# A two-layer graph kernel on one core: layer 0 of the first eight batches with plain weight blocks, factor sums of the q, k, v weights in other tiles, first loads from two queues

## The chip, the cores and the metric

The kernel runs on one core of a Trainium2 chip. The metric is the device time of one execution in microseconds (us); lower is better. A core has a matrix engine (TensorE, in the profile PE, with its weight loads shown as PEld), VectorE (DVE), ScalarE (ACT), GpSimd (POOL) and SyncE (SP). Each has its own queue of instructions and works through it strictly in order. SP does no arithmetic here: it issues transfers (DMAs), which 16 DMA engines carry out. An instruction that waits holds up everything behind it in its queue.

## The reference

128 batches of a 128x512 matrix go through two layers. `adj` is a 128x128 matrix shared by all batches.

```python
# layer 0
h = relu(layernorm(x))                                # x: (128, 128, 512) f32
x = x + (einsum('nm,bmd->bnd', adj, h) @ weight + bias)
# layer 1: masked attention with 8 heads of 64, projection, norm, two residuals
h = relu(layernorm(x))
q, k, v = split(h @ w_qkv)
p = softmax(where(adj == 0, -inf, q @ k.T / 8))
o = (p @ v) @ w_proj + b_proj
x = x + o + layernorm(o) * ln_gamma + ln_beta
```

All of it is float32.

## The kernel before

**Tiling.** A batch is one 128x512 tile. Layer 0 and the projection work on pairs of batches, the q, k, v products on groups of four, attention on single batches. The big products (`x @ weight`, `x @ w_qkv`, `x @ w_proj`) are done by a Strassen-Winograd scheme: the two-by-two block product takes seven block products instead of eight, and in return needs four sums of blocks on the left ("left factors", `left_factors`, on POOL: `ysum` for layer 0, `hsum` for q, k, v, `osum` for the projection) and four on the right ("factor sums" of the weights). `seven` runs the seven products as a generator, one per step of the plan. In layer 0 a block product is two matmuls of 128x128 by 128x256 for a pair of batches; in q, k, v it is four.

**The weights.** `w0_sb` and `wp_sb` hold seven blocks each, four loaded and three more, with one of the loaded ones overwritten, made by `combine_square` (four subtractions). The twelve factor sums of `w_qkv` do not stay in SBUF: `combine_qkv` loads the four blocks of one kind (q, k or v), forms four sums and writes them to DRAM (`SUMS`). `fetch` later brings the weight block of each product (a plain block from `w_qkv` or a sum from `SUMS`) into one of five `wq` buffers.

**The stages of a pair.** `load` (x into one of six buffers); `norm0` (statistics on DVE, a power on POOL, `relu` on ACT, and POOL adds the bias `b0` into x); `mix` (four small matmuls with the transposed `adj`, copied to `yT` by ACT); `pair_left`; `layer0` (seven products, results added to x by DVE straight from PSUM, giving x1); `norm1` (statistics, relu on ACT, then `exchange`: the tile goes to DRAM as `d` and comes back as `h1x` in four strips per batch, so that `flip`, a DVE transpose in 32x32 blocks, gives the full transpose `h1T`); `keep_x1` (POOL adds `beta`, SP stores x1 to DRAM); `group_left` and `qkv` for four batches; `scores`, softmax, a second exchange, `attend`, `project`, `finish`.

**What sets the order.** The order is written out by hand: `put(t, f, ...)` pushes every step with a key t on one heap, and the loop at the end pops the steps in order of t and emits their instructions. t is a planned time, but only the order matters: each engine gets its instructions in the order in which they are emitted. In the steady part a batch has a slot of 17.8 (`SLOT`, `when`). Slots below -3 (`BEGIN`) are squeezed to 7.0 each (`FILL`), which places the first layer 0 pairs, the sums of the weights and the loads ahead of slot 0. All transfers are issued by SP.

**The lines around the change.** Loads and weight blocks: L74, L81, L95, L98. `combine_square`: L102 to L105 (DVE for `w0_sb`, POOL for `wp_sb`). `combine_qkv`: loads L131, stores L136. `fetch`: L144. Power: L182. Exchange: out L195, back L200. Left factors: L209. Adding products from PSUM: L238 and L281. `relu` L249, bias L252, `mix` L261, layer 0 products L275, norm1's relu L300, `keep_x1` L307 and L309, `flip` L316, q, k, v products L344 with the copies L348, scores L364. The results of `combine_qkv` lie in tiles that attention uses later (`sx`, `pT`, `s`, `e`), the same ones for each of the three kinds.

Of the kernel before, what the change touches and what calls it, by code (L numbers as in the profile page):

```python
# [9 lines left out]
F32 = mybir.dt.float32  # L10
AF = mybir.ActivationFunctionType
ALU = mybir.AluOpType
AX = mybir.AxisListType

P = 128
# [5 lines left out]
def kernel(  # L21
# [71 lines left out]
    def load_square(w_sb, w):  # L93
        for k, row, col in ((0, 0, 0), (4, 0, F), (5, 1, 0), (3, 1, F)):
            nc.sync.dma_start(out=w_sb[:, k], in_=block(w, row, col))  # L95

    def broadcast(t, src):
        nc.sync.dma_start(out=t, in_=src.partition_broadcast(P))  # L98

    def combine(eng, b11, b12, b21, b22, t1, t2, t3, t4):  # L100

        eng.tensor_tensor(t1, b12, b11, op=ALU.subtract)  # L102
        eng.tensor_tensor(t2, b22, t1, op=ALU.subtract)
        eng.tensor_tensor(t3, b22, b12, op=ALU.subtract)
        eng.tensor_tensor(t4, b21, t2, op=ALU.subtract)  # L105
# [19 lines left out]
    def combine_qkv(t, kind):  # L125

        bs, ts = ([work.tile([P, 2, 2, F], F32, name=n, bufs=bufs) for n, bufs in names]
                  for names in ((("sx", 1), ("pT", 2)), (("s", 2), ("e", 1))))
        bs, ts = ([t_[:, n] for t_ in ts_ for n in range(2)] for ts_ in (bs, ts))
        for n, b in enumerate(bs):  # L130
            nc.sync.dma_start(out=b, in_=qkv_block(kind, n // 2, n % 2))  # L131

        def sums():
            combine(nc.vector, *bs, *ts)
            for k, t_ in zip((1, 2, 4, 6), ts):
                nc.sync.dma_start(out=SUMS[kind, k], in_=t_)  # L136

        put(t, sums)

    def fetch(g, kind, k):  # L140

# [129 lines left out]
    def pair_chain(left, w_sb, tiles, addend, x, y):  # L271

        def product(k, p, first, last):
            for c in range(2):
                nc.tensor.matmul(p[:, 0, :], lhsT=left[k][:, c, :], rhs=w_sb[:, k, c, :], start=first and c == 0,  # L275
                                 stop=last and c == 1, skip_group_check=True)

        results = [t[:, n * F:(n + 1) * F] for t in tiles for n in range(2)]

        def start(n, p):  # L280
            nc.vector.tensor_tensor(results[n], p[:, 0, :], addend[n // 2][:, n % 2 * F:(n % 2 + 1) * F], op=ALU.add)  # L281

        return seven({"x": x, "y": y, "z": "at"}, product, start, results, [1.0] * 7)

    def layer0(j):
        for b in (2 * j, 2 * j + 1):
# [29 lines left out]
        nc.vector.transpose(H1T[g][:, :, j, :].rearrange("p c (q r) -> p q c r", q=Q),  # L316
                            H1.pop(i).rearrange("p q (c r) -> p q c r", c=C))

    def group_left(g, t):

        h = H1T.pop(g)
        LEFT1[g] = left_factors(t, 4, h[:, 0:2, 0:2, :], h[:, 2:4, 0:2, :], h[:, 0:2, 2:4, :], h[:, 2:4, 2:4, :], "hsum")

    def qkv(g, kind):

# [121 lines left out]

    SLOT, FILL = 17.8, 7.0  # L450
    BEGIN, LAST = -3, B - G
    later, count = [], [0]

    def put(t, f, *a):
# [1 line left out]
        heapq.heappush(later, (t, count[0], f, a))  # L456

    def when(i, us):
        if i < BEGIN:
            return BEGIN * SLOT + (i - BEGIN + us / SLOT) * FILL  # L460
        return i * SLOT + us

    def run(make, times):

# [23 lines left out]
            return when(i, 0.5)  # L488
        return scores_at(i) + 3

    def h0_at(i):
        return when(i - 11 - i % 2, 13.2 if i % 2 else 12)

    def read_at(i):
        return when(i + 1, 9) if i < LAST and i % 2 else 0

# [16 lines left out]
    for i in range(-11, B):  # L513
        stage(when(i, 0), load, i + 13)
        t = when(i, (11.6, 9.2)[i % 2])
        stage(t, mix, i + 10, t)
        if i % 2:
            stage(t - 4, norm0, (i + 11) // 2, t - 4, bound=B // 2)
        if i >= 0:
            put(scores_at(i), scores, i, scores_at(i))  # L520
            put(flip_at(i), flip_probs, i)
            put(attend_at(i), attend, i, attend_at(i))

    idle = when(LAST, 13)
    for j in range(B // 2):
        a, b = 2 * j, 2 * j + 1
        i = a - 8
        t = when(i - 1, 12)
        put(t, pair_left, j, t, 2.5, YT, LEFT0, "ysum")
        run(lambda j=j: layer0(j), [when(i, p) for p in PAIR[0]])  # L530
        t = when(i, PAIR[0][6]) + 1.5
        put(t, norm1, j, t)
        put(when(i + 2, 7.5), flip, a)
        put(when(i + 2, 9), flip, b)
# [12 lines left out]
        put(end - 7, reload, a)  # L547
        put(end - 4, reload, b)
        put(end, finish, j, end)

    steps = []
    for g in range(B // G):
        i = g * G - 3
        put(when(i - 1, 13), group_left, g, when(i - 1, 13))
# [49 lines left out]
```

## Time and profile before

| what | value |
|---|---|
| time, median of 3 runs | 2447.01 us (2442.28 to 2448.1) |
| the profiled execution's own time | 2436.75 us |
| its span | 2435.0 us |
| busy: PE, PEld, DVE, ACT, POOL (us of the span) | 2338.9, 2051.1, 1617.8, 1043.9, 1681.7 |
| transfers on SP's queue | 521.89 MB, 66.9% of the 16 DMA engines' time |

All numbers but the first row come from one profiled execution. The page cuts the span into 40 slices: PE is at 90% or more in all of them but the first two and the last two. Idle time of another engine costs nothing by itself; idle time of PE does. The instructions in the rows are counted as the hardware runs them: a float32 matmul appears twice, so that one block product of layer 0 (two matmuls) is "x4" in a row and one of q, k, v (four matmuls) is "x8".

### The profile page before, as it was taken

The page shows a single profiled execution, that of the slowest core. Times are in us where ns is not written, and L with a number is a line of the kernel's source. Part 1 is how long each engine was busy: PE and PEld are TensorE (multiplying, and loading weights), DVE is VectorE, ACT ScalarE, POOL GpSimd, SP SyncE. Part 2 cuts the span into 40 slices and gives each one's busy share as a digit, 9 for nine tenths or more (in the row PEclk, how much of TensorE's full clock was granted, in tenths as well). Part 3 has the DMA queues.
Part 4 walks back from the last instruction along what each step waited for, and adds up shares of the span by engine and source line. Part 5 has one row for each costly group of instructions (what it writes and reads, how often), then busy time and mean ns, then how long its engine had stood idle before and what let it go on. Part 6 is the DMA issues. An engine that isn't in the chain of part 4 may idle for free.

```text
span 2435.0 us, 42720 instructions
## 1 busy us (share of the span) xinstructions
PE 2338.9 (96%) x14081; PEld 2051.1 (84%) x14081; DVE 1617.8 (66%) x3255; ACT 1043.9 (43%) x3074; POOL 1681.7 (69%) x1610
## 2 busy tenths in 40 slices
PE   4699999999999999999999999999999999999985
PEld 3588888888888888888888888888888888888873
DVE  4466667667667667677677677666766766766554
ACT  2144444444444444445444444444444444444432
POOL 3356776777867767867767777777777676776657
PEclk8899999999999999999999999999999999999998
DMA  4666776676677676667676676677667667667653
GB/s 161 212 217 217 229 225 216 222 227 214 227 228 221 221 226 215 221 224 224 219 230 215 222 228 219 215 227 230 216 221 228 224 210 229 219 217 227 207 161 109
DMA packets 400076, 524.62 MB, mean 215 GB/s; under 512 B 40048, under 2 KB 250096, under 8 KB 399856
## 3 DMA queue, kind: packets, MB, share of 16 engines
q1 hardware_dynamic: 399856, 521.89, 66.9%
q8 instruction: 113, 1.85, 0.3%
q14 instruction: 107, 0.88, 0.1%
HBM read 350.81 MB, written 170.92 MB: 214 GB/s over the span
## 4 chain that ended last, share of the span: by engine, by line
PE 88%; DMA 3%; DVE 3%; POOL 2%; issue 2%; SPq 1%; ACT 1%; POOLq 0%; DVEq 0%; ACTq 0%
PE pc L344 38%; PE pd L275 25%; PE pz L344 6%; PE ps L364 5%; PE po L411 5%; PE pmix L261 4%; PE pz L275 4%; DMA sx<-d 2%; SPq L200 1%; DVE pT L402 1%; ACT e L387 1%; DMA wq<-in_L_gnn_w_qkv_dram 0%; DMA pT<-in_L_gnn_w_qkv_dram 0%; DVE s L372 0%; DVE st L177 0%
## 5 line engine op out<-in xcount | busy, mean ns | idle before, releaser
L182 POOL TENSOR_TENSOR rs<-ve,minus_half 128x2 f32<-128x2 f32 x192 | 133.7, 696 | 660.8 <-DVE ve L180 573.4
L344 PE MATMUL pc<-hsum,wq 128*128 128x256 f32 x2048 | 485.1, 380 | 10.5 <-POOL hsum L209 5.3
L387 ACT ACTIVATE e<-s,mx 128x128 f32<-128x128 f32 x1024 | 397.0, 389 | 189.0 <-DVE mx L378 94.3
L344 PEld LDWEIGHTS pc<-hsum,wq 128*128 128x128 f32 x2048 | 388.8, 190 | 66.5 <-POOL hsum L209 6.9
L275 PE MATMUL pd<-w_sb,ysum 128*128 128x256 f32 x1024 | 267.8, 385 | 37.1 <-DVE x L281 31.5
L275 PE MATMUL pd<-wp_sb,osum 128*128 128x256 f32 x1024 | 265.7, 383 | 8.6 <-POOL osum L209 4.2
L396 POOL TENSOR_TENSOR e<-e,sm 128x1024 f32<-128x1024 f32 x128 | 244.9, 1913 | 29.8 <-DVE sm L395 24.1
L275 PEld LDWEIGHTS pd<-w_sb,ysum 128*128 128x128 f32 x1024 | 192.2, 193 | 63.9 <-issue 27.9
L344 PE MATMUL pc<-h1T,wq 128*128 128x256 f32 x1024 | 245.1, 382 | 0.0
L344 PE MATMUL pc<-wq,hsum 128*128 128x256 f32 x1024 | 244.9, 382 | 0.0
L574 ACT COPY oT<-po 128x512 f32<-128x512 f32 x128 | 74.9, 585 | 384.0 <-PE po L411 383.9
L402 DVE STREAM_TRANSPOSE pT<-sx 128x1024 f32<-128x1024 f32 x128 | 158.4, 1238 | 106.3 <-DMA sx<-d 106.3
L275 PEld LDWEIGHTS pd<-wp_sb,osum 128*128 128x128 f32 x1024 | 190.8, 192 | 35.1 <-POOL osum L209 7.3
L344 PEld LDWEIGHTS pc<-wq,hsum 128*128 128x128 f32 x1024 | 191.7, 190 | 29.2 <-ACT v L348 0.3
L344 PEld LDWEIGHTS pc<-h1T,wq 128*128 128x128 f32 x1024 | 191.9, 190 | 28.9 <-DMA wq<-in_L_gnn_w_qkv_dram 0.4
L372 DVE TENSOR_TENSOR s<-ps,maskb 128x512 f32<-128x512 f32 x256 | 159.2, 684 | 58.7 <-PE ps L364 58.7
L348 ACT COPY qkT<-pc 128x512 f32<-128x512 f32 x256 | 144.1, 574 | 118.9 <-PE pc L344 118.6
L437 ACT ACTIVATE t<-o,shift,rs 128x512 f32<-128x512 f32 x128 | 103.1, 807 | 206.6 <-DVE shift L186 204.9
L387 ACT ACTIVATION_READ_ACCUMULATOR e<-s,mx 128x1 f32 x1024 | 191.5, 187 | 0.0
L432 POOL TENSOR_TENSOR x1b<-x1b,o 128x512 f32<-128x512 f32 x128 | 162.7, 1271 | 21.1 <-DMA x1b<-x1d 19.1
L281 DVE TENSOR_TENSOR o<-pd,bp_b 128x256 f32<-128x256 f32 x256 | 106.3, 415 | 106.6 <-PE pd L275 106.1
L438 POOL TENSOR_TENSOR t<-t,gamma_b 128x512 f32<-128x512 f32 x128 | 162.9, 1272 | 18.7 <-ACT t L437 18.7
(83 smaller groups left out, 4702.6 us busy)
## 6 DMA issues: line engine op xcount, KB each, us to landing
wq<-wt SPq DMA_DIRECT2D x384, 256.0 KB, 3.8
wq<-in_L_gnn_w_qkv_dram SPq DMA_DIRECT2D x288, 256.0 KB, 3.5
d<-e SPq DMA_DIRECT2D x128, 512.0 KB, 2.9
sx<-d SPq DMA_DIRECT2D x512, 128.0 KB, 2.9
x<-in_x_dram SPq DMA_DIRECT2D x130, 256.0 KB, 4.3
d<-h SPq DMA_DIRECT2D x128, 256.0 KB, 2.9
x1d<-x SPq DMA_DIRECT2D x128, 256.0 KB, 3.1
h1x<-d SPq DMA_DIRECT2D x512, 64.0 KB, 2.2
```

Source lines behind the costliest of these rows:

```text
L182: nc.gpsimd.tensor_tensor(rs, ve, minus_half, op=ALU.pow)
L275: nc.tensor.matmul(p[:, 0, :], lhsT=left[k][:, c, :], rhs=w_sb[:, k, c, :], start=first and c == 0, stop=last and c == 1, skip_group_check ...
L344: nc.tensor.matmul(p[:, half, :], lhsT=lhsT, rhs=rhs, start=first and half == 0 and c == 0, stop=last and c == 1, skip_group_check=True)
L348: nc.scalar.copy(results[n], p)
L364: nc.tensor.matmul(ps[e][:, c, :], lhsT=qk[r, c, j % 2, :], rhs=qk[r, C + c, j % 2, :], start=True, stop=True)
L372: nc.vector.tensor_tensor(s[:, e * C:(e + 1) * C, :], ps[e], m4, op=ALU.add)
L387: nc.scalar.activation(e[:, :, h, :], s[:, h, :].rearrange("p (q r) -> p q r", q=Q), AF.Exp, bias=shift[:, h:h + 1], scale=scale, accum_ou ...
L396: nc.gpsimd.tensor_tensor(e, e, sm.unsqueeze(1).unsqueeze(3).to_broadcast([P, Q, H, R]), op=ALU.mult)
L402: nc.vector.transpose(PT[i].rearrange("p h (q r) -> p q h r", q=Q), S.pop(i).rearrange("p q (h r) -> p q h r", h=H))
L411: nc.tensor.matmul(p[e * HD:(e + 1) * HD, c, :], lhsT=v[:, h:h + HD], rhs=PT[i][:, e * C + c, :], start=True, stop=True)
L432: put(t + 1 + 3 * n, lambda i=i: nc.gpsimd.tensor_tensor(X1B[i], X1B[i], O[i], op=ALU.add))
L438: put(t + 1.5, lambda: nc.gpsimd.tensor_tensor(n, n, gamma_b, op=ALU.mult))
```

## The change

Layer 0 of batches 0 to 7 (`AHEAD = 8`) no longer goes through the seven products of a pair. A new function `layer0_whole` takes one batch at a time: eight matmuls with the four plain blocks of `weight` into one PSUM bank (`d0` or `d1` in turn), and a single 128x512 add on DVE. These batches need no left factors and no factor sums of `weight`, so `combine_square` of `w0_sb` moves from DVE at the start to POOL ahead of pair 4.

The plan's start is laid out anew: `START` is the key of the first `mix`, the eight batches follow at a `STEP` of 4.3, and slots below 0 are 9.6 long (`SHORT`). `combine_qkv` is split: the loads are emitted 12 ahead of the sums, each sum is a step of its own followed by its store, and each of the three kinds has its own tiles (kind 0 `sx`, `pT`, `s`, `e`; kind 1 `pT`, `s`, `o`; kind 2 `oT`, `x1b`, `t`). `adj`, the four blocks of `weight` and the bias are issued from ACT's queue instead of SP's. The load and the combination of `wp_sb`, and the broadcasts of `b_proj` and `gamma`, move from before slot 0 to slots 0 to 2. From batch 8 on, the keys of the stages are those of before.

```diff
-    nc.sync.dma_start(out=adj_sb, in_=adj)
+    nc.scalar.dma_start(out=adj_sb, in_=adj)
...
+    BLOCKS = (0, 4), (5, 3)
+    def load_square(eng, w_sb, w):
+        for row, places in enumerate(BLOCKS):
+            for col, k in enumerate(places):
+                eng.dma_start(out=w_sb[:, k], in_=block(w, row, col * F))
...
-    load_square(w0_sb, w0)
+    load_square(nc.scalar, w0_sb, w0)
     for i in range(2, 4):
         load(i)
-    broadcast(b0_b, b0)
+    broadcast(nc.scalar, b0_b, b0)
...
+    def load_qkv(kind, *names):
...
+        for n in range(4):
+            nc.sync.dma_start(out=pieces[n], in_=qkv_block(kind, n // 2, n % 2))
+        return pieces
+    def combine_qkv(eng, t, kind, pieces):
+        bs, ts = pieces[:4], pieces[4:8]
+        for n, (k, first, second) in enumerate(((1, 1, 0), (2, 3, None), (4, 3, 1), (6, 2, None))):
+            second = bs[second] if second is not None else ts[n // 2]
+            put(t + 1.5 * n, combine_one, eng, SUMS[kind, k], ts[n], bs[first], second)
+    def combine_one(eng, d, t, a, b):
+        eng.tensor_tensor(t, a, b, op=ALU.subtract)
+        nc.sync.dma_start(out=d, in_=t)
...
-            put(h0_at(i) + 2, bias, X[i])
+            put(h0_at(i) + (6 if i < AHEAD else 2), bias, X[i])
...
+    def layer0_whole(i, t):
+        p = psum.tile([P, 2, F], F32, tag=f"d{i % 2}", name=f"pd{i % 2}", bufs=1)
+        y = YT[i // 2] if i % 2 == 0 else YT.pop(i // 2)
+        for c in range(C):
+            for col in range(2):
+                nc.tensor.matmul(p[:, col, :], lhsT=y[:, c, i % 2, :], rhs=w0_sb[:, BLOCKS[c // 2][col], c % 2, :],
+                                 start=c == 0 and col == 0, stop=c == C - 1, skip_group_check=True)
+        X1[i] = work.tile([P, D], F32, name="x1", bufs=3)
+        put(t + 3.6, lambda: nc.vector.tensor_tensor(X1[i], p.rearrange("p a f -> p (a f)"), X.pop(i), op=ALU.add))
...
-    SLOT, FILL = 17.8, 7.0
-    BEGIN, LAST = -3, B - G
+    SLOT, SHORT, STEP = 17.8, 9.6, 4.3
+    BEGIN, LAST, AHEAD = -3, B - G, 8
+    START = BEGIN * SHORT - 38.5
...
+        return i * SLOT + us if i >= 0 else i * SHORT + us * SHORT / SLOT
+    def mix_at(i):
+        return START + i * STEP if i < AHEAD else when(i - 10, (11.6, 9.2)[i % 2])
+    def h0_at(i):
+        return mix_at(i) - 1.2 if i < AHEAD else when(i - 11 - i % 2, 13.2 if i % 2 else 12)
...
+            put(START - 3 + i if i < 6 else mix_at(i - 6) + 10 if i < AHEAD + 6 else when(i - 13, 0), load, i)
...
+        if a < AHEAD:
+            t = mix_at(a) - 5
+            put(t, norm0, j, t)
+            for n in (a, b):
+                t = mix_at(n) + 5.2
+                put(t, layer0_whole, n, t)
+            t += 4.4
+            flips = t + 11.7, t + 12.7
+        else:
...
+            put(t, pair_left, j, t, 2.5, YT, LEFT0, "ysum")
+            run(lambda j=j: layer0(j), [when(i, p) for p in PAIR[0]])
...
-    put(when(-10, 5), combine_square, nc.vector, w0_sb)
-    put(when(-10, 4), turn_adj)
-    put(when(-8, 16), make_mask)
-    for kind, t in enumerate((when(-9, 4), when(-4, 0), when(-2, 2))):
-        put(t, combine_qkv, t + 7, kind)
-    put(when(-6, 9), load_square, wp_sb, w_proj)
-    for t, src in ((beta_b, beta), (bp_b, b_proj), (gamma_b, gamma)):
-        put(when(-8, 9), broadcast, t, src)
-    put(when(-1, 9), combine_square, nc.gpsimd, wp_sb)
+    put(START - 6, turn_adj)
+    put(when(-2, 2), make_mask)
+    for kind, (t, tiles) in enumerate((
+            (START + 25, (("sx", 1, [P, Q, H * R]), ("pT", 2, [P, 2 * C, P]), ("s", 2, [P, 2 * C, P]), ("e", 1, [P, Q, H, R]))),
+            (START + 37, (("pT", 2, [P, 2 * C, P]), ("s", 2, [P, 2 * C, P])) + (("o", 4, [P, D]),) * 4),
+            (START + 48, (("oT", 2, [P, C, 2, P]),) * 2 + (("x1b", 2, [P, D]),) * 2 + (("t", 2, [P, D]),) * 2))):
+        put(t - 12, lambda kind=kind, t=t, tiles=tiles: combine_qkv(nc.vector, t, kind, load_qkv(kind, *tiles)))
+    put(when(-2, 9), combine_square, nc.gpsimd, w0_sb)
+    put(START + 8, broadcast, nc.sync, beta_b, beta)
+    put(when(0, 12), load_square, nc.sync, wp_sb, w_proj)
+    put(when(1, 3), broadcast, nc.sync, bp_b, b_proj)
+    put(when(1, 4), broadcast, nc.sync, gamma_b, gamma)
+    put(when(2, 12), combine_square, nc.gpsimd, wp_sb)
```

More of the change, by code (lines that the diff above doesn't have):

```diff
@@ L91, in block, with broadcast @@
         return w[row * F:(row + 1) * F, col:col + F].rearrange("(c p) o -> p c o", p=P)
[L93 to L98, printed above, removed]
+    BLOCKS = (0, 4), (5, 3)
[3 more added lines that the diff above has]
+                eng.dma_start(out=w_sb[:, k], in_=block(w, row, col * F))
+    def broadcast(eng, t, src):
+        eng.dma_start(out=t, in_=src.partition_broadcast(P))
     def combine(eng, b11, b12, b21, b22, t1, t2, t3, t4):
@@ L123 @@
     SUMS = {(kind, k): dram.tile([P, 2, F], F32, name=f"wt{kind}{k}", bufs=1) for kind in KINDS for k in (1, 2, 4, 6)}
[L125 to L138, printed above, removed]
+    def load_qkv(kind, *names):
+        pieces = []
+        for name, bufs, shape in names:
+            t = work.tile(shape, F32, name=name, bufs=bufs)
+            t = t if len(shape) == 2 else t.rearrange("p a b -> p (a b)") if len(shape) == 3 else \
+                t.rearrange("p a b c -> p (a b c)")
+            pieces += [t[:, n:n + D].rearrange("p (c o) -> p c o", c=2) for n in range(0, t.shape[1], D)]
+        for n in range(4):
[9 more added lines that the diff above has]
+        nc.sync.dma_start(out=d, in_=t)
     def fetch(g, kind, k):
@@ L317, in flip, with group_left @@
                             H1.pop(i).rearrange("p q (c r) -> p q c r", c=C))
-    def group_left(g, t):
+    def group_left(g, t, gap):
         h = H1T.pop(g)
-        LEFT1[g] = left_factors(t, 4, h[:, 0:2, 0:2, :], h[:, 2:4, 0:2, :], h[:, 0:2, 2:4, :], h[:, 2:4, 2:4, :], "hsum")
+        LEFT1[g] = left_factors(t, gap, h[:, 0:2, 0:2, :], h[:, 2:4, 0:2, :], h[:, 0:2, 2:4, :], h[:, 2:4, 2:4, :], "hsum")
     def qkv(g, kind):
@@ L458, in when @@
     def when(i, us):
-        if i < BEGIN:
-            return BEGIN * SLOT + (i - BEGIN + us / SLOT) * FILL
-        return i * SLOT + us
+        return i * SLOT + us if i >= 0 else i * SHORT + us * SHORT / SLOT
[3 more added lines that the diff above has]
+        return mix_at(i) - 1.2 if i < AHEAD else when(i - 11 - i % 2, 13.2 if i % 2 else 12)
     def run(make, times):
@@ L489, in softmax_at @@
         return scores_at(i) + 3
-    def h0_at(i):
-        return when(i - 11 - i % 2, 13.2 if i % 2 else 12)
     def read_at(i):
@@ L512 @@
     GROUP = (3.9, 6.5, 9.05, 13.3, 16.75), (1.5, 4.1, 6.7, 11.0, 14.4)
[L513 to L522, printed above, removed]
+    for i in range(B):
+        if i >= 4:
+            put(START - 3 + i if i < 6 else mix_at(i - 6) + 10 if i < AHEAD + 6 else when(i - 13, 0), load, i)
+        put(mix_at(i), mix, i, mix_at(i))
+        put(scores_at(i), scores, i, scores_at(i))
+        put(flip_at(i), flip_probs, i)
+        put(attend_at(i), attend, i, attend_at(i))
     idle = when(LAST, 13)
@@ L527 @@
         i = a - 8
[L528 to L531, printed above, removed]
+        if a < AHEAD:
[7 more added lines that the diff above has]
+        else:
+            t = when(i - 3, 5.2)
+            put(t, norm0, j, t)
+            t = when(i - 1, 12)
+            put(t, pair_left, j, t, 2.5, YT, LEFT0, "ysum")
+            run(lambda j=j: layer0(j), [when(i, p) for p in PAIR[0]])
+            t = when(i, PAIR[0][6]) + 1.5
+            flips = when(i + 2, 7.5), when(i + 2, 9)
         put(t, norm1, j, t)
-        put(when(i + 2, 7.5), flip, a)
-        put(when(i + 2, 9), flip, b)
+        put(flips[0], flip, a)
+        put(flips[1], flip, b)
         i = a + 5
@@ L553 @@
         i = g * G - 3
-        put(when(i - 1, 13), group_left, g, when(i - 1, 13))
+        t = when(i - 1, 13) if g else START + 36.2
+        put(t, group_left, g, t, 4 if g else 1.4)
         times = sorted(when(i + n, p) for n in range(G) for p in GROUP[(i + n) % 2] + ((13.1,) if n == 0 else ()))
```

## The prediction

> **What bounds the kernel now.** I read the stages first: busy time up to the first scores matmul, in the steady part, and at the end. Columns after the stretch: its length, busy time of PE, PEld, DVE, ACT, POOL with instruction counts, granted PE clock, DMA share, GB/s.
>
> ```profile
> 0.00:127.05 127.05, 75.59 (x323) 63.04 (x323) 54.50 (x123) 27.10 (x41) 48.27 (x55) 0.83 0.57 186
> 127.05:2300.00 2172.95, 2165.37 (x13180) 1909.71 (x13180) 1496.84 (x3003) 973.40 (x2887) 1552.52 (x1482) 1.00 0.69 221
> 2300.00:2435.00 135.00, 97.92 (x583) 78.31 (x581) 66.50 (x130) 43.45 (x146) 80.90 (x74) 0.91 0.45 147
> ```
>
> From 127.05 us to 2300 PE stands still for 7.6 us of 2173: PE is the bound, and an earlier start of this part moves everything behind it. Before 127.05 PE is busy 75.6 us, part of that at a lowered granted clock (0.83 on the mean). At the end another 37 us are idle, where the change moves nothing. So the question is when the first scores come (call it S; 127.05 now). The chain of waits shows that point:
>
> ```profile
> 122.70 0.89 PE pmix L261 x8
> 123.59 3.46 PE pc L344 x16
> 127.05 1.99 PE ps L364 x32
> ```
>
> Next the waits of the first 200 us, longest totals, and one of them in the timeline:
>
> ```profile
> PE pd L275 <- DVE x L281: 31.5, 4, 14.5
> DVE h1T L316 <- DMA h1x<-d: 25.9, 3, 14.5
> PEld pd L275 <- POOL ysum L209: 12.3, 4, 5.3
> ```
>
> ```profile
> 39.72 1.26 POOL L307 TENSOR_TENSOR x<-x,beta_b 128x512 f32<-128x512 f32 x1
> 40.93 0.73 POOL L209 TENSOR_TENSOR ysum<-yT,ysum 128x256 f32<-128x256 f32 x1
> 41.01 0.32 SPq L309 DMA_DIRECT2D x1d<-x  x1
> 41.42 3.72 SPq L200 DMA_DIRECT2D h1x<-d  x8
> ...
> 45.03 0.71 DVE L316 STREAM_TRANSPOSE h1T<-h1x 128x512 f32<-128x512 f32 x1 [10.59 <-DMA h1x<-d]
> 45.67 0.39 DVE L281 TENSOR_TENSOR x<-pd,x 128x256 f32<-128x256 f32 x1
> ...
> 46.20 2.04 PE L275 MATMUL pd<-w_sb,ysum 128*128 128x256 f32 x4 [9.78 <-DVE x L281]
> ```
>
> SP waits for POOL's `keep_x1` before it may issue the eight h1x strips; DVE has `flip` queued ahead of the add that frees PE's bank; PE waits 9.78 us. The same happens at 74.90 (14.5 us). So the start is a chain through DRAM and three queues, not PE work.
>
> **Part 1, the work PE must do before S.** The instruction orders of both programs put ten mixes and sixteen q, k, v products ahead of the first scores. Prices: mix 0.89, q/k/v product 1.73 (3.46 for x16), layer 0 product 0.86 (chain row at 130.96: "PE pd L275 x4" 0.86). Before: 10 x 0.89 + 28 x 0.865 + 16 x 1.73 = 60.8 us. After: the four pairs take eight products' worth instead of seven, 32 x 0.865 = 27.7 in place of 24.2, so 64.3. The plain blocks cost 3.5 us of PE.
>
> **Part 2, the first loads.** No transfer issued from ACT is in the trace; an issue costs 0.32 (x1d) to 0.47 (w_sb) on SP, and I take the upper. ACT issues `adj` and three weight blocks by 2.6. Its fourth block shares a completion semaphore with `adj`, the bias with the first block: with the median landing times of those rows (2.8 and 4.5 us after issue) ACT is free at about 6.2. Then come table load 1.28, adjT copy 0.25, first relu 0.81: first mix at 8.7, against 8.16 now. Cheapest issue: 0.9 earlier; so -0.4 to +0.5, with +0.5 taken. The two x tiles behind the first two leave SP 2.5 us earlier, but nobody is waiting for them so early.
> The Trainium skill, "DMA: Bandwidth & Descriptors", section "Issuing engines are not separate DMA queues", speaks against this part: loads issued from a second engine run on the same 16 DMA engines and save issue time alone. By the rule the part gains only SP's six issues (0.42 + 1.97 + 0.43 = 2.8 us of queue), by my rows it is half a microsecond late; I go by the rows.
>
> **Part 3, layer 0 of eight batches.** ACT now alternates relu and yT copy, so the second mix waits for the first copy: 8.7 + 1.9 (half of the 3.79 that the first two mixes take at 8.16, twice the steady 0.89) + 0.6 + 0.8, then 1.9 again gives 14.0. The first batch's matmuls, half of them still at that slow rate, 5.2: 19.2. From there PE is fed without a gap if each batch's other work stays below 0.89 + 3.46 = 4.35 us: ACT 0.81 + 0.59 + 0.81 = 2.2; POOL 1.27 + 1.27 + 0.70 = 3.2; DVE twice (0.69 + 0.18) plus 0.3 small ones plus one 128x512 add 0.69, plus flips and factor sums 1.0, is 3.8. All fit; DVE narrowly. Eight batches end at 19.2 + 6 x 0.89 + 7 x 3.46 = 48.8, call it 49.
> Do the flips still stop PE? The add of batch 1 ends at 24.3; norm1 (stats 1.9, power 0.7, shift, two relus) 29.1; two `keep_x1` on POOL 30.9; strips issued 31.2 to 35.0, each landing 2.3 later: flips end at 36.1 and 37.9. Behind the first flip stands the add of batch 4, whose matmuls end at 36.6, and PE needs its bank only for batch 6 at 41.8. So about 5 us of cover; without it each flip costs what it is late, at most the present 9.8 and 14.5.
>
> **Part 4, q and k of group 0.** The third and fourth flips wait for strips issued at 41 to 45.5, behind the four loads of kind 1, two sums and two stores: landing near 48, or 51 with the longer strip issues seen (6.12 us for eight at 66.66). Then hsum 1.27, a `keep_x1` 1.27 between, hsum 1.27: PE waits 5 to 8 us among the first products. By this path S = 49 + 16 x 1.73 + 2 x 0.89 + (5 to 8) = 83.5 to 86.5.
>
> **Part 5, the transfers, which I expect to decide.** Up to the weights of the second v product the new order issues 84 tiles of 262 KB (14 x, 2 broadcasts, 4 weight blocks, 12 qkv blocks, 12 sums stored, 8 d, 8 x1d, 32 strips worth 8, 16 wq) and `adj`: 22.1 MB. Some 3.2 MB go out before SP stops for the x buffer of batch 0 (free at 20); 18.9 MB remain, with another stop of 4 us for the first norm1. So the last lands at 24 + 18.9 MB / rate. Rates from 5 us stages:
>
> ```profile
> 10.00:15.00 5.00, 3.65 (x14) 2.75 (x12) 2.85 (x7) 1.17 (x2) 3.79 (x4) 1.00 1.01 364
> 65.00:70.00 5.00, 0.00 (x0) 0.00 (x0) 0.00 (x0) 0.00 (x0) 1.46 (x2) 0.50 0.93 295
> 105.00:110.00 5.00, 3.06 (x19) 2.60 (x17) 2.69 (x5) 1.17 (x2) 0.00 (x0) 1.00 0.90 316
> 110.00:115.00 5.00, 4.62 (x22) 4.11 (x23) 1.44 (x5) 0.58 (x1) 0.00 (x0) 1.00 0.80 263
> ```
>
> At 364 GB/s: 24 + 52 = 76, and part 4 decides (S = 83.5). At 270, the mean over 95 to 115 us (215, 288, 316, 263): 94, S = 96 after one more product. I take 300, near the full stages with mixed small pieces: 87, S = 89. The factor sums in separate tiles take their wait for earlier stores off DVE; their loads no longer block each other, which is why so much can be asked for in so short a time.
>
> **Part 6, behind S.** Four subtractions of `w_sb` on POOL, 4 x 1.28 = 5.1, stand before pair 4's left factors; POOL would be through them near 68 and with the left factors near 74, with pair 4 due after S + 3.7: hidden by 15 us or more, 5.1 if not. The same 5.1 for `wp_sb` now follow the third softmax division, where POOL now idles 9.9 us (up to 178.33): hidden, else 5.1. Four loads and two broadcasts, 1.6 MB and 2.8 us of SP, go out beside a DMA share of 69%: hidden, else 2.8. I take 1 us for all, 0 to 8 as bounds (one of the 5.1 and the 2.8). Otherwise the orders agree, so the 2308.0 us after S stay.
>
> **Sum.** Span 89 + 2308 + 1 = 2398, against 2435: 37 us less, of which PE's extra work already has been paid. The profiled execution took 2436.75, 10 us below the median of 2447.01; the difference is carried over: 2447 - 37 = 2410.
>
> **Rivals.**
> *The flips still stop PE.* For it: the store of x1 still stands ahead of the strips on SP, waiting for POOL, and flips still stand ahead of adds on DVE. Against it: a margin of 5 us, no left factors in between on POOL. If two stalls as long as now (24 us) came back, a third of that hidden behind the transfers, S = 105 and the time 2426.
> *The transfers never run faster than in the present start.* 186 GB/s is the mean up to 127.05. At that rate S = 24 + 102 + 1.7 = 127.5 and nothing is gained; that is the point from which it decides. At 165 (the window of 15 to 20 us has 164) S = 140, 13 us later; with 1 us behind S the time is 2461, slower. For it: SP is one queue in order with many small strips, and eight strips took 3.7 to 6.1 us for 0.5 MB. Against it: the present low mean is made of idle stages (0 GB/s in 30 to 35 and 55 to 60 us), while the full ones reach 263 to 364.
> *Faster transfers than I think*, S = 83.5 and no loss behind it: 2447 - 44.5 = 2402.5. It lies in the forecast's own range.
> *The change does less than it says* (the ACT loads late): part 2 bounds that at 0.5 us.
>
> **How the numbers follow.** Forecast, S from 83.5 to 96: 0.70, time 2410, own range 2402 to 2424 (S = 96 and 8 us behind it: 2447 - 23). Flips: 0.23, at 2426. Slow transfers: 0.07, of which 0.03 lands near no change and 0.04 above. The three runs spread from -4.7 to +1.1 around their median, so the range is 2398 to 2428. About 0.3% (7.3 us) is what a measurement can tell from no change: faster 0.93, same 0.03, slower 0.04.
>
> **What would show it.** In the new profile the first scores should come at 84 to 96 us, PE should be nearly full from about 14 to 49 us at clock 1.00 soon after the start, DMA should carry 270 GB/s or more from 27 us on, and the waits of "PE pd <- DVE x" should be down from 31.5 us to a few. I am wrong if flips are named again ahead of long PE waits, if the new part after S idles more than 16 us, or if wq waits hold PE while the DMA share is low (then SP's order, not the rate, decides).

## The result and the profile after

| | before | after |
|---|---|---|
| time, median (lowest to highest), 4 runs each | 2445.62 us (2442.28 to 2448.1) | 2411.27 us (2403.35 to 2413.47) |
| the profiled execution: time, span | 2436.75, 2435.0 us | 2413.47, 2411.7 us |
| first scores (S) in it, by the chain | 127.05 us | 94.66 us |
| span behind S in it | 2308.0 us | 2317.0 us |

The ratio after to before is 0.9855, 95% interval 0.9829 to 0.988. The time was forecast at 2410, S at 89.

The stages of the new kernel, in the columns used before (length; busy time of PE, PEld, DVE, ACT, POOL; granted PE clock; DMA share; GB/s):

```profile
0.00:94.66 94.66, 72.86 (x339) 61.51 (x339) 53.12 (x101) 27.11 (x41) 46.10 (x46) 0.96 0.75 244
94.66:2270.00 2175.34, 2164.25 (x13161) 1906.80 (x13160) 1491.39 (x3000) 973.06 (x2886) 1546.67 (x1477) 1.00 0.69 221
2270.00:2411.70 141.70, 104.80 (x600) 84.01 (x600) 67.54 (x131) 44.12 (x147) 85.12 (x77) 0.88 0.46 147
```

The first stage is 32.4 us shorter, although PE is busy in it for 72.9 us, nearly as long as before (75.6): the gain came out of idle PE time. The steady part is PE bound as before: 11.1 us idle of 2175.

The waits of the first 200 us (total, times, longest):

```profile
DVE h1T L338 <- DMA h1x<-d: 5.5, 6, 2.6
PE pc L366 <- POOL hsum L220: 4.4, 3, 2.5
PE pc L366 <- POOL x L329: 4.4, 1, 4.4
PE pd L302 <- DVE x L305: 3.1, 1, 3.1
```

PE's wait for the add in layer 0 fell from 31.5 us to 3.1, and DVE's wait for the strips from 25.9 to 5.5. What is left sits among the q, k, v products. The timeline of PE (start, duration; in brackets the idle time before the row and what ended it):

```profile
7.94 2.08 PE L272 MATMUL pmix<-adjT,h 128*128 128x128 f32 x8 [3.38 <-ACT h L260]
...
47.02 3.69 PE L302 MATMUL pd<-w_sb,yT 128*128 128x256 f32 x16 [3.12 <-DVE x L305]
50.54 1.89 PE L366 MATMUL pc<-h1T,wq 128*128 128x256 f32 x8
54.92 2.65 PE L366 MATMUL pc<-hsum,wq 128*128 128x256 f32 x8 [2.49 <-POOL hsum L220]
...
66.74 3.46 PE L366 MATMUL pc<-hsum,wq 128*128 128x256 f32 x8 [4.37 <-POOL x L329]
...
77.48 1.96 PE L366 MATMUL pc<-hsum,wq 128*128 128x256 f32 x8 [1.25 <-DMA wq<-wt]
...
83.17 3.69 PE L366 MATMUL pc<-hsum,wq 128*128 128x256 f32 x16 [1.11 <-DMA wq<-in_L_gnn_w_qkv_dram]
...
94.59 2.06 PE L386 MATMUL ps<-qkT 64*128 64x128 f32 x32
```

Layer 0 ends at 50.5. From there 16 products of 1.73 and two mixes of 0.89 make 29.5 us of work, and S would come at 80. It came 14.6 us later. About 10 are the waits of these rows and smaller ones of the same kind. Most of the rest are slow products behind a wait: the one at 66.74 takes 3.46 us where 1.89 is usual in these rows, in a window whose granted clock is 0.66.

The wait at 66.74 is put down to POOL, but SP's timeline, with rows of ACT and DVE of the same time, shows weight fetches that came late:

```profile
58.65 3.34 SPq L211 DMA_DIRECT2D h1x<-d  x4
62.38 0.34 SPq L155 DMA_DIRECT2D wq<-wt  x1
63.29 1.52 ACT L322 ACTIVATE h<-x,shift,rs 128x512 f32<-128x512 f32 x2 [5.09 <-DVE shift L197]
64.72 0.56 ACT L370 COPY qkT<-pc 128x512 f32<-128x512 f32 x1
...
71.20 0.91 SPq L155 DMA_DIRECT2D wq<-wt  x2
...
76.01 1.76 DVE L148 TENSOR_TENSOR x1b<-oT,x1b 128x512 f32<-128x512 f32 x1
76.23 2.53 SPq L211 DMA_DIRECT2D h1x<-d  x4
78.86 0.38 SPq L149 DMA_DIRECT2D wt<-x1b  x1
79.33 0.40 SPq L155 DMA_DIRECT2D wq<-in_L_gnn_w_qkv_dram  x1
```

The fetch for the product at 66.74, the fifth, was issued at 62.38, behind four strips, and the chain of waits has its transfer as 4.22 us long, so it landed at 66.60. It is not the only thing that this product waits for: ACT's copy of an earlier product stands behind two relus of the last of the four pairs and ends at 65.28, and in the experiments in which the block is there in time, the same product waits 2.6 to 3.2 us for this copy (e1, e9, e10, e11). Of the 4.37 us, then, about 3 would be left without the late fetch. The product at 77.48 waits for one of the two fetches from 71.20, whose transfer took 6.14 us. The fetch for the product at 83.17 stands at 79.33, behind four strips that are being issued until 78.76 and the store of a sum, which DVE had finished at 77.77. SP's queue in order holds the fetches. But the transfer engines were full as well, as 5 us windows show:

```profile
15.00:20.00 5.00, 5.00 (x28) 4.54 (x27) 2.03 (x4) 1.25 (x2) 0.00 (x0) 1.00 0.08 11
...
40.00:45.00 5.00, 3.90 (x20) 3.13 (x19) 2.42 (x2) 0.58 (x1) 1.87 (x2) 1.00 1.05 392
...
60.00:65.00 5.00, 2.36 (x11) 1.73 (x10) 3.10 (x9) 1.71 (x3) 4.20 (x4) 1.00 0.97 330
65.00:70.00 5.00, 3.26 (x8) 2.52 (x8) 2.06 (x4) 1.79 (x3) 2.40 (x3) 0.66 0.92 288
```

From 30 to 85 us they carry 291 GB/s on the mean. Whether data or order set S, and what the nearly idle transfers from 10 to 20 us (36 GB/s) cost, is what the experiments ask.

### The profile page after: what moved, and what is told of

Its sections match the earlier page's. It is cut to its first block, busy times and chain, and to the rows that moved or that the text cites. A ratio compares the mean times of both kernels' runs of the same rounds, so it can differ in the third digit from the quotient of the medians.

```text
span 2411.7 us, 42673 instructions
## 1 busy us (share of the span) xinstructions
PE 2341.9 (97%) x14097; PEld 2052.3 (85%) x14097; DVE 1612.0 (67%) x3231; ACT 1044.3 (43%) x3074; POOL 1677.9 (70%) x1598
## 4 chain that ended last, share of the span: by engine, by line
PE 84%; DMA 5%; POOL 3%; DVE 3%; issue 2%; SPq 2%; ACT 1%; POOLq 0%; DVEq 0%; ACTq 0%
PE pc L366 37%; PE pd L286 23%; PE pz L366 6%; PE ps L386 5%; PE po L433 5%; PE pmix L272 4%; PE pz L286 4%; DMA sx<-d 2%; SPq L211 1%; DMA wq<-wt 1%; DVE pT L424 1%; POOL x1b L454 1%; POOL t L460 1%; POOL t L464 1%; DMA wq<-in_L_gnn_w_qkv_dram 1%
## 5 line engine op out<-in xcount | busy, mean ns | idle before, releaser
L286 PE MATMUL pd<-w_sb,ysum 128*128 128x256 f32 x960 | 246.3, 379 | 0.0
L286 PEld LDWEIGHTS pd<-w_sb,ysum 128*128 128x128 f32 x960 | 177.9, 190 | 21.7
L454 POOL TENSOR_TENSOR x1b<-x1b,o 128x512 f32<-128x512 f32 x128 | 162.7, 1271 | 35.5 <-DMA x1b<-x1d 33.4
L188 DVE BATCH_NORM_STATS2 st<-x 128x6 f32<-128x512 f32 x256 | 172.1, 672 | 3.0 <-DMA x<-in_x_dram 2.9
```

The source lines that it names most:

```text
L188: nc.vector.bn_stats(st, src)
L454: put(t + 1 + 3 * n, lambda i=i: nc.gpsimd.tensor_tensor(X1B[i], X1B[i], O[i], op=ALU.add))
```

## The experiments

S below is the start of the first scores matmul in the profiled execution of each run (126.98 before, 94.59 after). All ratios are to the kernel before on the same chip, so they can be compared across chips; its median there was 2448.4 us for the first four experiments, 2448.01 for the next four and 2451.46 for the last four.

| run | S, us | time, us | ratio (95%) |
|---|---|---|---|
| after | 94.6 | 2411.27 | 0.9855 (0.9829 to 0.988) |
| e0_again | 94.1 | 2417.4 | 0.9864 (0.9841 to 0.9886) |
| e1_early_loads | 89.9 | 2413.14 | 0.9849 (0.9825 to 0.9873) |
| e2_x1_four | 96.3 | 2416.86 | 0.9867 (0.9847 to 0.9886) |
| e3_seven_products | 102.4 | 2424.63 | 0.9899 (0.9881 to 0.9916) |
| e4_data_twice | 99.9 | 2421.75 | 0.9888 (0.9863 to 0.9913) |
| e5_issues_twice | 95.7 | 2418.34 | 0.9883 (0.9856 to 0.991) |
| e6_same_tiles | 105.6 | 2427.58 | 0.992 (0.9896 to 0.9945) |
| e7_first_from_sync | 94.1 | 2420.95 | 0.9879 (0.9844 to 0.9914) |
| e8_before_again | 130.4 | 2447.98 | 0.999 (0.997 to 1.001) |
| e9_no_fetch | 89.1 | 2411.24 | 0.984 (0.9805 to 0.9875) |
| e10_no_fetch_early | 85.9 | 2409.28 | 0.9829 (0.98 to 0.9858) |
| e11_no_fetch_early_x | 85.2 | 2406.1 | 0.9814 (0.9783 to 0.9844) |

The intervals of neighbours overlap, so S, a number of one trace, decides between theories, and the time confirms only large steps.

S itself carries a spread from the start. The first batch's matmuls in layer 0 took 4.35 to 5.72 us in the executions with plain blocks, and SP's queue goes on only when their add has freed the first x buffer: at 18.65 and 18.57 us in the two of the changed kernel, at 20.03 in e2, 19.88 in e4, 19.03 in e5, 19.16 in e6, 18.04 in e7 and 20.02 in e9. Counted from there, S lies at 75.9 and 75.5 us in the changed kernel, and at 76.3, 80.0, 76.6, 86.5, 76.0 and 69.1 in these six. So a difference of up to 2 us between two values of S can be the start alone.

### The changed kernel once more

No edit; it asks whether the 9 us that the span behind S grew between the two first profiles are a loss or spread.

> The changed kernel once more, nothing altered. In its first profile the first scores matmul starts at 94.6 us, 32.4 us earlier than before, but its span is only 23.3 us shorter than that of the profile of before. Theory A: the start is the same in every execution and the rest is spread of single executions behind the first scores: the scores start at 94.6 again within 0.5 us, the time lies between 2403 and 2414, and the ratio to the kernel before stays near 0.986. Theory B: the change costs some 9 us behind the first scores in every execution: the lead of 32.4 us at the first scores is again down to about 24 us at the last ones.

S came at 94.08 and the span was 2418.3, so 2324.2 lie behind S, against 2317.1 by the same measure in the profile above. One kernel differs by 7 us between two executions, with the same instructions.

### The loads of the weight blocks earlier

```diff
-        put(t - 12, lambda kind=kind, ...: combine_qkv(...))
+        put(START + 3 + 0.4 * kind, lambda kind=kind, ...: combine_qkv(...))
```

> All twelve loads of the q, k, v blocks are issued right behind the sixth x tile, ahead of the x tile that waits for a free buffer, so that they go out between 8 and 19 us, where the DMA engines moved 61 and 11 GB/s. Theory A (the amount of data after 20 us decides when the first scores come): eight of the twelve used to go out between 35 and 58 us; 2.1 MB less there at 300 GB/s is 7 us: scores at 86 to 89 us, time some 6 to 8 us below the changed kernel. Rival B (SyncE's order decides: weight fetches stand behind the stores of the factor sums and behind strips that wait): only eight issues of 0.46 us leave the queue: scores at 91 to 94, time 1 to 3 us lower. Rival C (neither, PE's chain from layer 0 decides): scores at 94 to 95, no change.

S came at 89.90, 4.2 to 4.7 us earlier. In 10 us windows the transfers moved forward:

```profile
10.00:20.00 10.00, 8.65 (x35) 7.61 (x36) 1.08 (x2) 2.86 (x5) 2.49 (x2) 1.00 1.06 341
20.00:30.00 10.00, 10.00 (x56) 9.02 (x55) 7.14 (x18) 4.60 (x8) 5.15 (x6) 1.00 0.22 79
...
40.00:50.00 10.00, 10.00 (x51) 8.46 (x49) 7.00 (x11) 2.12 (x4) 5.43 (x5) 1.00 0.85 276
```

PE's timeline has this wait at the fifth product:

```profile
64.47 3.25 PE L366 MATMUL pc<-hsum,wq 128*128 128x256 f32 x8 [3.18 <-ACT qkT L370]
```

Between 10 and 20 us they now carry 341 GB/s where the changed kernel had 36. PE is full from 40 to 50 us as well (6.88 of 10 there in the changed kernel): with less queued at that time, the x1 store that held the add no longer came late. Moving data forward brings S forward, which speaks for the transfers. It does not bring all of it: PE still waits 3.89 us for the left factors, and 3.18 at the fifth product, now for ACT's copy (63.80 to 64.36), which stands behind the relus of the last pair. So S lies between the ranges of the two theories.

### A fourth buffer for x1

```diff
-X1[i] = work.tile([P, D], F32, name="x1", bufs=3)
+X1[i] = work.tile([P, D], F32, name="x1", bufs=4)
```

> x1 gets four buffers in place of three. In the changed kernel the add of batch 5 waits 3.75 us for the store of an earlier x1 to land, and PE waits 3.1 us for that add at 47.0. With four buffers this wait should be gone in every theory and layer 0 of the eight batches end near 47.4 instead of 50.5. Theory A (data after 20 us decides): first scores stay at 93.5 to 95, time unchanged within 1.5 us. Rival C (PE's chain from layer 0 through the flips decides): scores at 91 to 92, time 3 us lower.

The 3.1 us wait in layer 0 was gone and its last row ended at 48.73 instead of 50.71, but S came at 96.29, not earlier; counted from where SP's queue goes on, it is 0.3 to 0.8 us later than in the changed kernel. The timeline of PE shows where the time went:

```profile
55.95 8.47 PE L366 MATMUL pc<-hsum,wq 128*128 128x256 f32 x24 [4.80 <-DMA wq<-in_L_gnn_w_qkv_dram]
67.66 2.52 PE L366 MATMUL pc<-hsum,wq 128*128 128x256 f32 x8 [3.24 <-DMA wq<-wt]
```

Waits for weights take the place of the wait for the buffer. The theory that PE's own chain through layer 0 sets S falls with this: what a shorter layer 0 gains is lost again within the first products.

### Seven products again in the new order

The pairs of the first eight batches go through the seven products again, with left factors and `combine_square` on DVE at the start, in the new plan. x1 has four buffers here. The keys of the loads of x and of group 0's left factors move a little too (not shown below), and with them the four loads of kind 0 go out at 7.7 to 11 us instead of 19 to 21, so the transfers are not quite those of the changed kernel.

```diff
-            for n in (a, b):
-                t = mix_at(n) + 5.2
-                put(t, layer0_whole, n, t)
-            t += 4.4
+            t = mix_at(b) + 2
+            put(t, pair_left, j, t, 0.8, YT, LEFT0, "ysum")
+            run(lambda j=j: layer0(j), [mix_at(b) + 4 + 1.23 * k for k in range(7)])
+            t = mix_at(b) + 13
...
-    put(when(-2, 9), combine_square, nc.gpsimd, w0_sb)
+    put(START - 1, combine_square, nc.vector, w0_sb)
```

> The dense plan of the start stays, with the loads, the tiles and the queues of the change, but layer 0 of the first eight batches goes through the seven products of a pair again (factor sums of the weight on VectorE at the start, left factors on GpSimd, adds from PSUM by VectorE; x1 has four buffers, which a pair needs). Theory A (the plain blocks are what lets PE run without waits at the start): left factors and the chain of adds come back, PE waits several us per pair, four pairs take 50 us or more instead of 37, first scores at 103 to 115, time 2420 to 2432. Rival D (the denser plan alone makes the gain; the plain blocks only cost their 3.5 us of PE): scores at 91 to 95, time 2408 to 2412.

S came at 102.42: 7.8 us later than with plain blocks, though PE has 3.5 us less work by the prediction's count. This is a little less than the range given for it. Its timeline has eight waits for DVE's adds in layer 0, 11.0 us together, this the longest:

```profile
51.48 2.07 PE L286 MATMUL pd<-w_sb,yT 128*128 128x256 f32 x4 [3.58 <-DVE x L249]
```

Seven products need more additions, of 256 columns each, and DVE does not keep up with them. So the plain blocks are worth some 8 of the 32 us in this plan, and the new order and tiles the rest.

### Eight weight transfers twice, with their data and without

The eight loads of kinds 1 and 2 are each followed by another transfer on SP that nobody reads: the whole block to a DRAM tile, or, in the second kernel, a corner of 16x2x8 to SBUF, which has the issue and next to no data.

```diff
             nc.sync.dma_start(out=pieces[n], in_=qkv_block(kind, n // 2, n % 2))
+            if kind:
+                nc.sync.dma_start(out=extra[4 * kind - 4 + n], in_=qkv_block(kind, n // 2, n % 2))
```

> Each of the eight block loads of kinds 1 and 2 is followed on SyncE by a second transfer of the same 256 KB block from DRAM into a DRAM buffer that nothing reads: 2.1 MB more between 35 and 58 us and eight more issues. Theory A (the amount of data decides when the first scores come; they stand at 94.1 and 94.6 us in two profiles of the changed kernel): 2.1 MB at 300 GB/s is 7 us: scores at 100 to 103, time 6 to 8 us up. Rival B (SyncE's issues and its order decide): eight issues of 0.46 us: scores at 97 to 99, time 3 to 4 us up. Rival C (neither): 94 to 95.

> The same eight additional issues in the same places, but each moves 1 KB only (16 partitions of 64 bytes, into tiles that nothing reads). Theory A (data): scores at 94 to 95.5, time unchanged within 1.5 us. Rival B (issues and order of the queue): 97 to 99, 3 to 4 us up, as in the run with the whole blocks.

With the data S came at 99.92, with the issues alone at 95.67; the changed kernel has 94.59 and 94.08, and nothing of the computation is left out in either. So the eight issues cost 1.1 to 1.6 us and 2.1 MB of data about 4.2 more; counted from where SP's queue goes on, 0.7 to 1.1 and 3.4. At the 291 GB/s measured, 2.1 MB take 7.2 us: about half of it reaches S. In the kernel with the data PE's wait in layer 0 is longer (5.31 us instead of 3.12), and the fifth product waits for its fetch again, 6.1 us later than before:

```profile
72.87 3.75 PE L370 MATMUL pc<-hsum,wq 128*128 128x256 f32 x8 [7.03 <-DMA wq<-wt]
```

The data is the larger part; the issue slots on SP are a smaller one, near the 0.5 us between the two executions of the changed kernel.

### The same tiles for all three kinds

The new plan keeps, but kinds 1 and 2 use kind 0's tiles (`sx`, `pT`, `s`, `e`), as in the kernel before.

```diff
-            (START + 37, (("pT", 2, ...), ("s", 2, ...)) + (("o", 4, [P, D]),) * 4),
-            (START + 48, (("oT", 2, ...),) * 2 + (("x1b", 2, [P, D]),) * 2 + (("t", 2, [P, D]),) * 2))):
+            (START + 37, (("sx", 1, ...), ("pT", 2, ...), ("s", 2, ...), ("e", 1, ...))),
+            (START + 48, (("sx", 1, ...), ("pT", 2, ...), ("s", 2, ...), ("e", 1, ...))))):
```

> The three kinds use the same tiles again (sx, pT, s, e), so the loads of a kind wait on SyncE until the sums of the kind before have read these tiles; all else as changed. Theory F (the tiles of their own keep SyncE from stopping): SyncE stands from 35 to about 42 us and again from 55 to about 62, the strips of the first exchange behind it; first scores at 102 to 110, time 8 to 15 us up. Rival G (the queue is bound by the data anyway and makes it up): scores at 94 to 97, at most 2 us up.

S came at 105.62, 11 us later, and the time confirms it (2427.58 us). SP's and PE's rows:

```profile
41.28 0.91 SPq L138 DMA_DIRECT2D sx<-in_L_gnn_w_qkv_dram  x2
...
66.80 0.90 SPq L138 DMA_DIRECT2D sx<-in_L_gnn_w_qkv_dram  x2
...
73.38 0.34 SPq L155 DMA_DIRECT2D wq<-wt  x1
...
78.14 3.75 PE L366 MATMUL pc<-hsum,wq 128*128 128x256 f32 x8 [11.61 <-DMA wq<-wt]
```

The loads of kind 1 wait for the sums of kind 0 to leave their tiles, and they stand on SP, so everything behind them waits too: SP issues nothing between 35.5 and 41.3 nor, for kind 2, between 59.1 and 66.8, and 40 to 60 us carry 266 GB/s instead of 315. The fetch of the fifth product goes out at 73.38 instead of 62.38. The other tiles are the largest single part found, 11 us. With the 8 of the plain blocks that leaves some 13 of the 32 us for the new order, which no run takes out by itself.

### The first loads from SP

```diff
-    nc.scalar.dma_start(out=adj_sb, in_=adj)
+    nc.sync.dma_start(out=adj_sb, in_=adj)
...
-    load_square(nc.scalar, w0_sb, w0)
+    load_square(nc.sync, w0_sb, w0)
...
-    broadcast(nc.scalar, b0_b, b0)
+    broadcast(nc.sync, b0_b, b0)
```

> adj, the four blocks of the layer 0 weight and the bias are issued by SyncE again, all else as changed. The first mix started at 8.16 us in the kernel before and at 7.94 in the changed one. Theory H (the second queue is worth next to nothing, since nobody waits for these loads): first mix between 7.5 and 8.3, first scores at 94 to 95.5, time unchanged within 1.5 us. Rival I (SyncE's 2.8 us of six issues delay what comes behind): scores at 96 to 98, 2 to 3 us up.

S came at 94.08, the same as with ACT issuing. The first mix is even earlier; the timeline of this kernel:

```profile
7.33 2.08 PE L272 MATMUL pmix<-adjT,h 128*128 128x128 f32 x8 [1.95 <-ACT h L260]
...
0.73 1.28 ACT L167 ACT_TABLE_LOAD   x1 [0.73 <-PEq L630]
```

and that of the changed kernel:

```profile
1.17 3.19 ACTq L99 DMA_DIRECT2D w_sb<-in_L_gnn_weight_dram  x4
...
5.61 1.28 ACT L167 ACT_TABLE_LOAD   x1 [5.61 <-DMA w_sb<-in_L_gnn_weight_dram]
```

When ACT issues the loads, its table load of 1.28 us stands behind them at 5.61 and is on the path to the first mix, which comes at 7.94 instead of 7.33. The Trainium skill, "DMA: Bandwidth & Descriptors", section "Issuing engines are not separate DMA queues", says that a second issuing engine saves issue time only; here no gain of that kind shows at S.

### The kernel before once more

No edit; it asks where a second execution of the kernel before has its S and how much lies behind it.

> The kernel before once more, nothing altered, for a second profile. In its first profile the first scores start at 127.0 us and 2308 us follow. Theory J (the start repeats, the stretch behind the first scores varies by some 10 us from one execution to the next in both kernels, about 2320 on the mean): scores at 126 to 128, and with a time near 2448 the rest is 2316 to 2324. Rival K (the stretch behind is 2308 in the kernel before and some 10 us longer in the changed one): the rest is 2306 to 2311 again.

S came at 130.36 and 2320.5 us lie behind it, where the first profile had 126.98 and 2308.0. Both long waits of layer 0 are there again in its timeline:

```profile
47.60 2.04 PE L275 MATMUL pd<-w_sb,ysum 128*128 128x256 f32 x4 [10.85 <-DVE x L281]
...
75.20 2.04 PE L275 MATMUL pd<-w_sb,ysum 128*128 128x256 f32 x4 [14.22 <-DVE x L281]
```

So the first profile of the kernel before was a short execution, by 3.4 us ahead of S and 12.5 behind it, and the "9 us more behind S" come from the comparison with it: 2320.5 is what the changed kernel has too.

### Without the fetches of the first group

The blocks and sums of group 0 are used where `combine_qkv` has them, so 21 fetches are not issued; the sums are still stored for the later groups. The second kernel adds the early loads, the third also the four x1 buffers and later loads of x for batches 10 to 13.

```diff
         bs, ts = pieces[:4], pieces[4:8]
+        for k, piece in enumerate((bs[0], ts[0], ts[1], bs[3], ts[2], bs[2], ts[3])):
+            WQ[0, kind, k] = piece
...
-        put(steps[n - 4][0] + 0.1 if n >= 4 else t - 10, fetch, *a)
+        if a[0]:
+            put(steps[n - 4][0] + 0.1, fetch, *a)
```

> Group 0 takes its weight blocks straight from the tiles in which combine_qkv has them (the four loaded blocks and the four sums, which now have tiles of their own); its 21 fetches fall away, 16 of them ahead of the first scores: 4.2 MB and 16 issues less on SyncE between 43 and 93 us. The stores of the sums stay, for the later groups. Theory A (the amount of data after 20 us decides, and with it the wait of a product for its block): the waits for wq at 66, 70, 77 and 83 us go, scores at 84 to 88 us, time 7 to 10 us below the changed kernel. Rival L (flips, left factors on GpSimd and copies decide): scores at 91 to 94, time up to 3 us lower.

> The kernel without fetches for group 0 and with the twelve loads of the q, k, v blocks issued behind the sixth x tile, so that 6.3 MB of the 18.9 MB leave the stretch from 20 to 94 us. Theory A: data no longer decides; PE's own chain does: layer 0 to 48, some 5 us of waits for the third and fourth flip and the left factors, 16 products and two mixes of 29.5 us: scores at 80 to 84, time 12 to 15 us below the changed kernel. Rival L: no more than the run with early loads alone, scores at 89 to 91.

> As the run before, and the loads of batches 10 to 13 are issued 13 to 20 us of the plan later, and x1 has four buffers, so that the third and fourth strips meet less traffic and PE does not wait for the store of x1. Theory A with data no longer deciding: 1 MB less between 40 and 60 us gains little: scores within 2 us of the run before. Rival M (the strips of batches 2 and 3 still queue behind other data): scores 3 to 5 us earlier than in the run before.

S came at 89.09, 85.87 and 85.19. Without fetches it is 5.0 to 5.5 us earlier, with early loads besides 8.2 to 8.7, a little less than the two gains together (9.2 to 10.2). In the second kernel no wait for weights is left ahead of S:

```profile
52.25 1.99 PE L368 MATMUL pc<-hsum,s 128*128 128x256 f32 x8 [2.25 <-POOL hsum L222]
55.15 1.99 PE L368 MATMUL pc<-hsum,s 128*128 128x256 f32 x8 [0.91 <-POOL hsum L222]
...
61.76 3.40 PE L368 MATMUL pc<-hsum,e 128*128 128x256 f32 x8 [2.89 <-ACT qkT L372]
```

What remains are the left factors (3.2 us) and ACT's copy (2.9), and S is where the prediction's path without transfers had it (83.5 to 86.5), though that path has no wait for the copy. The third kernel has the lowest median of all, 2406.1 us. It beats the kernel before clearly. Against the changed kernel its interval (0.9783 to 0.9844) still overlaps that of 0.9855, so that step (5 us between the medians, 10 us by the ratios) is likely and not proved by the times; S, 9 us earlier, is the firmer sign.

## Why the prediction was right, and where it was not

The time was 1 us off and S 5.6 us late, so the closeness is partly luck; step by step:

**Part 1 and part 3, layer 0.** PE's work and the fit of the other engines held: PE is full from 15 to 40 us (5.00 of 5 in every window). The first batch was done at 17.66 instead of 19.2 (17.05 to 19.04 in the other executions of this layer 0). The flips did not stop PE: they ended at 36.9 and 39.7 and stood ahead of no late add. A wait that was not in the sum came instead: three x1 buffers, so the add of batch 5 waited for a store issued at 40.22, and PE 3.1 us behind it. End 50.5, forecast 49. The second experiment shows no gain at S without it.

**Part 2, the ACT loads.** First mix 7.94 and, in the second execution, 8.06: forecast 8.7, and 8.16 in both executions of before, so it is 0.1 to 0.2 earlier than before and not 0.5 later. ACT went on at 5.61, not at 6.2. Against the same plan with SP issuing (7.33) ACT's issues do cost 0.6. At S neither is seen.

**Part 4, the path through the left factors.** Forecast 83.5 to 86.5 for S by this path alone, with 5 to 8 us of waits. Once the fetches were gone and the loads early, S came at 85.2 and 85.9 with 4.9 and 6.1 us of waits. The sum held, its terms only in part: the left factors made 2.4 and 3.2 us of it, and 2.6 and 2.9 were ACT's copy behind the relus of the last pair, which this part does not name.

**Part 5, the transfers.** They decide, as forecast, and the rate was nearly right (300 assumed, 291 measured from 30 to 85 us). The end of the stream was nearly right too:

```profile
20.00:88.80 68.80, 55.87 (x261) 46.79 (x260) 45.69 (x81) 17.95 (x28) 38.05 (x31) 0.95 0.86 277
```

That is 19.1 MB, so the 18.9 MB of the sum were through at about 88 us, forecast 87. The step that was mis-sized is the next one, S "after one more product": it takes the transfers as one stream that PE follows to its end. In fact the last block for which PE waited landed at 83.03, and six products and a mix, 11.4 us, stood behind it. The fetches are spread through SP's queue, each behind strips, loads or stores, and each late one stops PE by itself (1.25 and 1.11 us, some 1.4 of the 4.37 beyond ACT's copy, and the slow products behind such waits). From 83.17 on PE is full until S, so nothing of it is made up. S was 5.6 us late, and without the fetches it came 5.0 to 5.5 us earlier. The prediction had named "wq waits hold PE while the DMA share is low" as the sign of SP's order; the share was high at the long wait (0.92 to 0.97) and only 0.64 in 75 to 80 us, so both count: for eight more transfers the data 3 to 4 us and the issues about 1.

**Part 6, behind S.** Forecast 1 us lost, 0 to 8 as bounds. Behind S lie 2314.5 to 2327.1 us in eight profiled executions (the changed kernel twice, and the experiments e1, e2 and e4 to e7), 2308.0 and 2320.5 in the two of the kernel before. The ranges overlap, so no loss is shown; one of about 5 us could not be told from this spread. Counted from S = 130.4, the time gained is 3 to 9 us less than S gained in the first eight experiments, and equal to it within 3 us in the last three.

**The sum.** The prediction carried over 10 us from the short profile of before to the median; its 2436.75 us lie below every timed run of that kernel on record (lowest 2442.28). With S at 130.4 in a usual execution, the step is 130.4 - 94.6 = 35.8 us, beside 34.4 us between the medians of the four runs (35.7 from the 2447.01 of the prediction). S came 5.6 later than forecast, and S of before is 3.4 later in a usual execution than the one taken; the two errors cancel in good part.

**The rivals.** Flips that still stop PE: not seen. Transfers at 186 GB/s: not seen, 244 on the mean up to S. S of 83.5: reached only without the fetches and nearly so.

## What to carry over

When several steps share one queue that issues in order, do not price transfers as bytes over rate alone: look for the fetch that the next product needs and ask what stands ahead of it, above all strips of other stages and loads into tiles that are not free; and ask how much work of the engine stands behind the last late block. Tiles of their own were worth 11 us here, layer 0 with plain blocks 8, although it is more work for PE, and a second issuing engine nothing. A wait that is removed ahead of a stage bound by transfers comes back there, as the fourth x1 buffer showed. And take the start of a stage from two executions before counting on a difference of a few microseconds.

## What the runs showed of the hardware

In the first 100 us of the changed kernel, DVE subtractions with both operands in SBUF took 0.65 to 0.69 us where POOL's operation had ended or began later, and 1.13 to 1.76 where one of POOL's tensor operations was under way. DVE's and POOL's rows of the changed kernel:

```profile
53.09 0.65 DVE L148 TENSOR_TENSOR o<-pT 128x512 f32<-128x512 f32 x1
53.25 1.62 POOL L220 TENSOR_TENSOR hsum<-h1T 128x512 f32<-128x512 f32 x1 [0.29 <-DVE h1T L338]
53.78 1.64 DVE L148 TENSOR_TENSOR o<-s,o 128x512 f32<-128x512 f32 x1
54.83 1.71 POOL L329 TENSOR_TENSOR x<-x,beta_b 128x512 f32<-128x512 f32 x1
```

The second subtraction starts at 53.78 while POOL's sum runs until 54.87, and ends at 55.42, 0.55 us after that; POOL's next addition is then 1.71 instead of 1.27. The adds of L305, which read one operand from PSUM, stayed at 0.65 to 0.69; the one at 31.27 took 0.69 beside a POOL addition that ran from 31.02 to 32.29. The Trainium skill, "SBUF — State Buffer", section "Who interferes with whom", describes such a port pair of VectorE and GpSimd as an exclusive lock that makes the later one wait; these rows agree with it. The prediction put flips and factor sums together at 1.0 us of DVE a batch; what the longer subtractions cost at S was not tried.

The span behind S differs by some 10 us between executions of the same instructions. No run here shows why.
